# Statistics of the norm ahead of layer 1's router: row sum from the operation that makes x, variance by ScalarE's square with bias and sum

## The chip, the cores and the metric

The kernel runs on 1 core of one Trainium2 chip. The metric is the device time of one execution in microseconds (us). Each kernel is run several times and the median counts. The profile is of one further execution, whose own time is given beside its span. Engines are named as the profile names them: PE (matmul, with PEld for its weight loads), DVE (VectorE), ACT (ScalarE), POOL (GpSimd), SP (SyncE, which here only issues DMAs).

## The reference, cut to what matters

Two layers, each a graph attention over N = 2708 nodes with D = 256 features, followed by a mixture of experts in which each node goes to its two best experts. Layer 1 is the part that matters here:

```
x = x + L1_gnn(layernorm(x), adj, ...)        # out: 2708 x 256
n = layernorm(x)                              # (x - mean) / sqrt(var + 1e-5), per row
logits = n @ gate_w                           # 256 x 16 experts
top-2 experts and their softmax weights
moe = sum over both of weight * (relu(n @ w1[e]) @ w2[e])     # w1: 256 x 512, w2: 512 x 256
x = x + layernorm(n + moe) * gamma + beta
```

The change is in the second line: how the mean and the variance of a row of the new x are found.

## The kernel before, in words

The 2708 rows are 22 tiles of up to 128 rows (tiles 20 and 21 have 74). In layer 1 the attention is a product on PE: for each tile 44 matmuls at `att_ps` (L1772) with the mask, widened from 8 bits by POOL (L1620) or ACT (L1622), as weights. The order of tiles on PE is 20, 2 to 19, 21, after 0 and 1.

Around this product a planner orders everything at build time. `Clock` holds a list of generators ("pieces"). A piece yields an engine and an estimated time, or a `Mark` that another piece sets; `Clock.run` always lets the piece with the earliest start go on, and the order in which it does so is the order of instructions on every engine. On the chip each engine takes its instructions strictly in that order, and waits where an operand is not there yet. So a change of a piece's estimates or waits can move other pieces' instructions on every engine.

The pieces that matter here:

- `attention` issues the matmuls of L1772. A tile needs one of three accumulators, which `finish1` of an earlier tile gives back.
- `finish1(t)`: `inv` (L1982, DVE reads the sum from the accumulator), three activations (L1985, L1987, L1989, ACT), two DVE operations (L1991, L1993; the second frees the accumulator), and a square with sum (L1997, ACT).
- `points1(part)`: works on a part of tiles at once: (0-3), (4-5), (6-9), (10-11), (12-15), (16-17), (18-19), (20-21). Some fifty small DVE operations on 128 x n numbers (L379 to L396, about 0.2 us each when one waits for the other) with activations L2011, L2061, L2063 and L2070 between; then per tile the new x (L2090, DVE, 128 x 256) and its statistics (`ln_f1.stats`: `bn_stats` L481 and `bn_aggr` L482, DVE); then per part `var` (L379), nine steps of a reciprocal square root, `shift` (L391), and per tile the normalized row `xr` (L506, ACT), which is stored (L1020, a DMA by SP).
- `logits1(two)`: transposes of `xr` on PE (L515), a copy (L610, ACT), the gate product (L520, PE), and `logits` (L626, DVE).
- `route1(group)`, groups of tiles (0-5), (6-11), (12-17), (18-21): the top two per row (L648 to L667, DVE), ranks (L680 to L690, PE), numbering (L710 to L746, DVE), then `scatter1`, two indirect DMAs per tile by POOL that move `xr` to its experts' rows (L753), and `plan`, which finds which expert each block of 128 rows has (L881 to L948: `where` L925 by ACT, `hot_f` L933 by DVE, `bias_ps` L943 by PE). After the groups 1, 2 and 3 a plan is made; blocks 0 to 7 can start after group 1, blocks 8 to 19 after group 2.
- `stream`: 45 blocks of experts. SP fetches the block's rows (L850) and weights (L834, L838) in its own order, in which the stores of L1020 stand too. PE: transposes (L515), 16 steps of weight load and matmul at `hid_ps` (L972), and at `out_ps` (L987, L990). ACT: the copy `lo` (L1108) and four `ht` (L976). DVE: `yo` (L996). POOL adds `yo` to the sums in memory by an indirect DMA (L1001). PE's transposes, gate products and ranks of the last groups stand between the steps of the first blocks.

Before the change the part's statistics are these lines:

```
nc.vector.scalar_tensor_tensor(x1[:r, t, :], emb[:r, t, :], by[:r, q:q + 1], xq[q][:r, :D],
                               op0=OP.mult, op1=OP.add)
ln_f1.stats(x1[:r, t, :], t, r)
...
var = ts(ln_f1.mv[:, lo:hi, 1], LN_EPS, OP.add)
yield from rsqrt_steps(var, dev)
shift = ln_f1.shift(part)
```

Of the kernel before, what the change touches and what calls it, by code (L numbers as in the profile page):

```python
# [16 lines left out]
AF = mybir.ActivationFunctionType  # L17
OP = mybir.AluOpType
# [5 lines left out]
LN_EPS = 1e-5  # L24
# [123 lines left out]
def kernel(  # L148
# [25 lines left out]
    nc = tc.nc  # L174

    ctx.enter_context(tc.manual_schedule(engines={ET.PE, ET.Activation, ET.DVE, ET.SP}))
    N, D = x.shape
# [88 lines left out]
    def xr0_tile():  # L266
        return lasting.tile([P, RW], F32, name="xr", bufs=5)
# [95 lines left out]
    def stat(n, dtype=F32):  # L363

        count[0] += 1
        cols, bufs = next(of for of in STATS if n <= of[0])
        return sm.tile([P, cols], dtype, name=f"stat{count[0]}", tag=f"stat{cols}",
                       bufs=bufs)[:, :n]

    def kept(name, fill=None, cols=T):  # L370
        tl = sm.tile([P, cols], F32, name=name)
        if fill is not None:
            nc.gpsimd.memset(tl, fill)
        return tl

    def ts(a, s1, op0, s2=None, op1=None, dtype=F32):
        o = stat(a.shape[1], dtype)
        if op1 is None:
            nc.vector.tensor_scalar(o, a, s1, None, op0=op0)  # L379
        else:  # L380
            nc.vector.tensor_scalar(o, a, s1, s2, op0=op0, op1=op1)
        return o

    def tt(a, b, op, o=None):
        o = stat(a.shape[1]) if o is None else o
        nc.vector.tensor_tensor(o, a, b, op)
        return o

    def sts(a, s, op0, b, op1, o=None):
        o = stat(a.shape[1]) if o is None else o  # L390
        nc.vector.scalar_tensor_tensor(o, a, s, b, op0=op0, op1=op1)  # L391
        return o

    def recip(a):
        o = stat(a.shape[1])
        nc.vector.reciprocal(o, a)  # L396
        return o
# [6 lines left out]
    SMALL = "DVE", 0.11, 0.09  # L404
# [9 lines left out]
    def rsqrt_steps(v, o=None):  # L414

        yield SMALL
        shifted = ts(v.bitcast(I32), 1, OP.logical_shift_right, dtype=I32)
        yield SMALL
        y = ts(shifted, -1.0, OP.mult, float(0x5F3759DF), OP.add, dtype=I32).bitcast(F32)
        yield SMALL  # L420
        r = tt(v, y, OP.mult)
        yield SMALL
        r = tt(r, y, OP.mult)
        yield SMALL
        h = sts(r, -10.0 / 3.0, OP.add, r, OP.mult)
        yield SMALL
        y = sts(h, 5.0, OP.add, y, OP.mult)
        c = 0.375
        yield SMALL
        h = sts(v, -0.5 * c ** 3, OP.mult, y, OP.mult)  # L430
        yield SMALL
        h = tt(h, y, OP.mult)
        yield SMALL
        return sts(h, 1.5 * c, OP.add, y, OP.mult, o)
# [1193 lines left out]
    def xr_tile():  # L1628
        return side.tile([P, RW], F32, name="xr1", bufs=13)

    def fetch_row(tl, src, t, r):
        for lo, hi in parts_of_rows(r):
            nc.sync.dma_start(tl[lo:hi], src[t * P + lo:t * P + hi, :])
# [218 lines left out]

    emb = h_all[:, :, :D]
    emb_sq, sig_sq, common = kept("emb_sq", 1.0), kept("sig_sq", 32.0), kept("common")
    router1 = Router(1, E1, groups1, wg1, bg1, side)
    router1.fill()
    sums1 = [sums_d(f"sums1_{k}", zero=k == 1) for k in range(2)]
# [8 lines left out]
    x1 = emb  # L1866
    square = side.tile([P, D], BF16, name="square")
    ln_f1, ln_y = Norm("f1"), Norm("y")

    clock = Clock()  # L1870
# [14 lines left out]
    def group_of(two):  # L1885
        return next(g for g in groups1 if g[0][0] <= two[0][0] <= g[-1][0])

    def urgency(two):
        return 1 + groups1.index(group_of(two)) / len(groups1)
# [139 lines left out]
    def points1(part):  # L2029

        lo, n = part[0][0], len(part)
        hi = lo + n
        xq, xp_slots, x_at = [], [], [Mark() for _ in range(n // 2)]

        def fetch_x():
            for k in range(0, n, 2):
                xp_slots.append((yield from xps.get()))
                for t, r in part[k:k + 2]:
                    xq.append(xr0_tile())
                    fetch_row(xq[-1][:, :D], x_d, t, r)  # L2040
                clock.moved(x_at[k // 2], 0.9, 2.0)

        sq = emb_sq[:, lo:hi]
        v = stat(2 * n)
        yield SMALL
        nc.vector.tensor_scalar(v[:, :n], sq, MIN_NORM * MIN_NORM, None, op0=OP.max)
        yield SMALL
        nc.vector.tensor_scalar(v[:, n:], sq, 1.0, None, op0=OP.add)
        y = yield from rsqrt_steps(v)
        yield SMALL  # L2050
        roots = tt(v, y, OP.mult)
        yield SMALL
        u = tt(roots[:, :n], roots[:, n:], OP.add)
        log = yield from half_log(u)
        yield SMALL
        clock.start(fetch_x())
        inward = sts(log, 0.5 * LEAST, OP.max, y[:, :n], OP.mult)

        for q, (t, r) in enumerate(part):
            yield "ACT", 0.5  # L2060
            nc.scalar.activation(emb[:r, t, 1:], emb[:r, t, 1:], AF.Tanh, scale=inward[:r, q:q + 1])  # L2061
            yield "ACT", 0.7
            nc.scalar.activation(square[:r, 1:], emb[:r, t, 1:], AF.Square,  # L2063
                                 scale=0.5, bias=half[:r], accum_out=sig_sq[:r, t:t + 1])

        y = yield from rsqrt_steps(sig_sq[:, lo:hi])
        yield SMALL
        s_n, e = tt(sig_sq[:, lo:hi], y, OP.mult), stat(n)
        yield "ACT", 0.22
        nc.scalar.activation(e, s_n, AF.Exp)  # L2070
        yield SMALL
        ie = recip(e)
        yield SMALL
        sinh = tt(e, ie, OP.subtract)
        by = common[:, lo:hi]
        yield SMALL
        nc.vector.scalar_tensor_tensor(by, sinh, 0.25, y, op0=OP.mult, op1=OP.mult)
        yield SMALL
        cosh = tt(e, ie, OP.add)
        yield SMALL  # L2080
        ratio = recip(by)
        yield SMALL
        ratio = sts(cosh, 0.5, OP.mult, ratio, OP.mult)
        yield SMALL
        nc.vector.tensor_scalar(emb[:, lo:hi, 0], ratio, -1.0, None, op0=OP.add)
        for q, (t, r) in enumerate(part):
            if q % 2 == 0:
                yield x_at[q // 2]
            yield "DVE", 0.5
            nc.vector.scalar_tensor_tensor(x1[:r, t, :], emb[:r, t, :], by[:r, q:q + 1], xq[q][:r, :D],  # L2090
                                           op0=OP.mult, op1=OP.add)
            yield "DVE", 0.62
            ln_f1.stats(x1[:r, t, :], t, r)
            if q % 2:
                clock.set(xp_slots[q // 2])
        dev = ln_f1.rstd[:, lo:hi]
        yield SMALL
        var = ts(ln_f1.mv[:, lo:hi, 1], LN_EPS, OP.add)
        yield from rsqrt_steps(var, dev)
        yield SMALL  # L2100
        shift = ln_f1.shift(part)
        for q, (t, r) in enumerate(part):
            xr_slots[t] = yield from xrs.get()
            router1.rows[t] = xr_tile()
            yield "ACT", 0.6
            ln_f1.apply_s(router1.rows[t][:r, :D], x1[:r, t, :], t, r, shift[:, q:q + 1])
            experts1.store(t, r, router1.rows[t][:r, :D])
            if q % 2:
                clock.start(logits1(part[q - 1:q + 1], taken_at[t - 1]), urgency(part))
        if hi == group_of(part)[-1][0] + 1:  # L2110
            clock.start(route1(group_of(part)), urgency(part))

    def route1(group):
        g = groups1.index(group)
        for t, _ in group[::2]:
            yield taken_at[t]
        if g:
            yield routed_at[g - 1]
        yield from router1.pick(group, 0)
        yield from router1.pick(group, 1)  # L2120
        slot = yield from bank.get()
        yield "PE", 0.16 * len(group)
        router1.rank(group)
        yield from router1.number(group)
        clock.set(slot)
        upto = experts1.NB if group is groups1[-1] else early1.get(g)
        clock.start(scatter1(group, upto), urgency(group))
        if upto:
            yield from experts1.plan(upto, bank)
        clock.set(routed_at[g])  # L2130

    def scatter1(group, upto):
        for t, r in group:
            yield "POOL", 2.6
            router1.scatter(t, r)
            clock.set(xr_slots.pop(t))
        if upto:
            clock.set(experts1.scattered_at[upto], 3.5)
# [362 lines left out]
```

## Time and profile before

| what | value |
|---|---|
| median of 3 runs | 1139.43 us (1137.65 to 1140.55) |
| the profiled execution | 1135.28 us, of it the span 1133.6 us |
| PE busy | 1038.0 us (92%) |
| DVE busy | 542.4 us (48%) |
| ACT busy | 576.4 us (51%) |
| POOL busy | 368.5 us (33%) |
| layer 1's attention, 740 to 871 us: PE busy | 114.41 of 131 us |
| the change-over to the experts, 871 to 946 us: PE busy | 50.87 of 75 us |
| experts, 946 to 1105 us: PE busy | 152.07 of 159 us |

A row of the timeline gives start, duration, engine, line, operation, output and inputs, and in brackets how long the engine had been idle before it and what ended that. "Issue" is idle time that no recorded wait explains; "remote" is a wait for another engine whose work had long ended by the record. A row of the table of windows gives the stretch, its length, and for each engine its busy time (and instructions), then the granted clock of PE, the busy share of the DMA engines and GB/s. Shares of busy time over the whole span say little here: before 740 us other parts of the program run, which the change does not touch.

### The profile page before, as it was taken

Reading aid. Unit: us, or ns where it says so; the run is one execution under the profiler, and the core shown is the slowest. Engines: PE = TensorE matmul, PEld = TensorE weight load, DVE = VectorE, ACT = ScalarE, POOL = GpSimd, SP = SyncE. Lnnn points to the kernel's source line nnn. Section 1 sums busy time; section 2 is a strip of 40 time slices with the busy share of each in tenths; the row PEclk is TensorE's granted clock in tenths of the full one; section 3 lists DMA queues with packets and bytes.
Section 4 is the critical chain, followed back from the end, with each engine's and each line's share of the span. In section 5 each row is a group of like instructions: output and inputs, shape, how many; then the busy total and the mean of one; then the engine's idle time right before and its main releaser. Section 6 shows DMA issues by size and latency. Waiting matters only on the chain. (4 is left out here: it accounts for less than half of the span.)

```text
span 1133.6 us, 21472 instructions
## 1 busy us (share of the span) xinstructions
PE 1038.0 (92%) x6707; PEld 921.6 (81%) x6707; DVE 542.4 (48%) x2210; ACT 576.4 (51%) x1602; POOL 368.5 (33%) x425
## 2 busy tenths in 40 slices
PE   5999999998989999999999999898985967999994
PEld 3788888887879999998999854898984856999882
DVE  7778888887421111101110347577865553122257
ACT  4866667664524444444444346545653633544454
POOL 7531112111242222112213361352534155434350
PEclk9999999999999999999999999997996788999997
DMA  9965454431889999999899959401114656785893
GB/s 289 282 248 177 137 176 152 170 95 55 306 252 283 331 323 321 325 305 319 257 312 331 356 155 279 160 1 51 53 61 130 179 138 144 162 203 105 227 292 129
DMA packets 161862, 234.38 MB, mean 207 GB/s; under 512 B 10891, under 2 KB 137798, under 8 KB 159032
## 3 DMA queue, kind: packets, MB, share of 16 engines
q1 hardware_dynamic: 143356, 209.90, 57.0%
q0 software_dynamic: 18384, 23.03, 10.6%
q8 instruction: 56, 0.92, 0.3%
q14 instruction: 66, 0.54, 0.2%
HBM read 205.54 MB, written 54.59 MB: 229 GB/s over the span
## 5 line engine op out<-in xcount | busy, mean ns | idle before, releaser
L996 DVE TENSOR_SCALAR yo<-out_ps,w 128x256 f32<-128x256 f32 x89 | 43.0, 483 | 383.3 <-PE out_ps L990 376.2
L1346 PE MATMUL att_ps<-g_all,z 128*128 128x257 f32 (+3 forms) x968 | 223.6, 383 | 0.0
L1346 PEld LDWEIGHTS att_ps<-g_all,z 128*128 128x128 f32 (+3 forms) x968 | 174.9, 186 | 29.5 <-issue 2.9
L990 PE MATMUL out_ps<-room,ht 128*128 128x256 f32 x840 | 191.4, 380 | 0.0
L972 PEld LDWEIGHTS hid_ps<-xt,room 128*128 128x128 f32 x1504 | 176.9, 194 | 9.3 <-issue 3.7
L972 PE MATMUL hid_ps<-xt,room 128*128 128x128 f32 x1504 | 178.9, 278 | 5.4 <-issue 2.7
L990 PEld LDWEIGHTS out_ps<-room,ht 128*128 128x128 f32 x840 | 155.5, 191 | 20.0
L1332 ACT ACTIVATE zr<-e_bc,minus_one,g_all 128x256 f32<-128x256 f32 (+3 forms) x242 | 130.2, 591 | 44.4 <-DVE z L1335 44.3
L1772 PE MATMUL att_ps<-half,wide_mask 128*128 128x258 f32 (+1 forms) x962 | 131.3, 295 | 14.9 <-issue 8.1
L976 ACT ACTIVATE ht<-hid_ps,w_t 128x128 f32<-128x128 f32 x376 | 128.6, 364 | 30.3 <-PE hid_ps L972 11.7
L1001 POOL DMA_INDIRECT sums<-yo,xg x43 | 66.8, 1554 | 233.8 <-DVE side L964 188.5
L1772 PEld LDWEIGHTS att_ps<-half,wide_mask 128*128 128x128 f32 (+1 forms) x962 | 124.5, 198 | 19.0 <-issue 14.8
L753 POOL DMA_INDIRECT rows_d<-xr,place x88 | 91.8, 1043 | 119.7 <-DVE xr L497 66.4
L1335 DVE SCALAR_TENSOR_TENSOR z<-zr,mask_t 128x256 f32<-128x256 f32 (+3 forms) x242 | 97.8, 424 | 31.1 <-ACT zr L1332 17.4
L976 ACT ACTIVATE ht<-hid_ps,w1x 128x128 f32<-128x128 f32 x180 | 65.1, 366 | 83.5 <-PE hid_ps L972 67.5
L1001 POOL DMA_INDIRECT sums<-yo,xr x42 | 65.7, 1564 | 117.0 <-DMA sums<-yo,xr 40.6
L966 ACT ACTIVATE w<-xg,side 128x1 f32<-128x1 f32 x43 | 12.7, 294 | 165.8 <-DVE side L964 165.8
L1620 POOL CAST wide_mask<-mask_t 128x1408 fp32r<-128x1408 fp8e4 x34 | 47.0, 1387 | 95.8 <-PE att_ps L1772 95.8
L972 PE MATMUL hid_ps<-lo,wide_mask 128*128 128x128 f32 x368 | 51.2, 297 | 3.5 <-ACT lo L1108 3.0
L972 PEld LDWEIGHTS hid_ps<-lo,wide_mask 128*128 128x128 f32 x368 | 49.5, 211 | 5.7 <-ACT lo L1108 3.9
L515 PE MATMUL tr_ps<-ident,xr 128*128 128x128 f32 (+1 forms) x214 | 39.6, 297 | 14.6 <-ACT xr L506 12.9
L515 PEld LDWEIGHTS tr_ps<-ident,xr 128*128 128x128 f32 (+1 forms) x214 | 28.1, 154 | 22.1 <-ACT xr L506 14.2
(334 smaller groups left out, 1442.6 us busy)
## 6 DMA issues: line engine op xcount, KB each, us to landing
room<-in_L_ffn_W_dram SPq DMA_DIRECT2D x94, 1024.0 KB
room<-in_adj_dram SPq DMA_DIRECT2D x20, 1354.0 KB
wide_mask<-in_L_ffn_w_dram SPq DMA_DIRECT2D x46, 512.0 KB
room<-in_L_ffn_w_dram SPq DMA_DIRECT2D x22, 512.0 KB
mask_t<-in_L_ffn_w_dram SPq DMA_DIRECT2D x22, 512.0 KB
rows_d<-nobody SPq DMA_DIRECT2D x1, 7511.0 KB
rows_d<-nobody SPq DMA_DIRECT2D x5, 1295.0 KB
sums<-nobody SPq DMA_DIRECT2D x2, 2944.0 KB
```

Source lines behind the costliest of these rows:

```text
L515: nc.tensor.transpose(ps[:, c, :r], src[:, c * P:(c + 1) * P], ident[:r, :r])
L753: ins = nc.gpsimd.indirect_dma_start(out=self.rows_d[:, :], in_=self.rows[t][:r], in_offset=None, out_offset=bass.IndirectOffsetOnAxis(ap= ...
L972: nc.tensor.matmul(ps[:, :P], w1_b[:, c, f * P:(f + 1) * P], xt[:, c, :], start=(c == 0), stop=(c == DC - 1))
L976: nc.scalar.activation(ht[:, f, :], ps[:, :P], self.func, bias=self.bias[:, f, b:b + 1])
L990: nc.tensor.matmul(ps[:, :D], ht[:, f, :], self.rooms[b % self.deep][1][:, f, :], start=False, stop=(f == self.FC - 1))
L996: nc.vector.tensor_scalar(yo, ps[:, :D], w, None, op0=OP.mult)
L1001: ins = nc.gpsimd.indirect_dma_start(out=self.sums[k][:, :], in_=yo, in_offset=None, out_offset=bass.IndirectOffsetOnAxis(ap=self.rows.pop ...
L1332: nc.scalar.activation(zr[:k, :n], e_bc[:k, lo:lo + n], AF.Relu, bias=minus_one[:k], scale=g_all[:k, j, D + 1:D + 2])
L1335: nc.vector.scalar_tensor_tensor(z[:k, :n], zr[:k, :n], 1.0, mask_t[:k, j // 2, lo:lo + n, j % 2], op0=OP.add, op1=OP.mult)
L1346: nc.tensor.matmul(accs[i][:r, :D + 1], z[:k, q * P:q * P + r], g_all[:k, j, :D + 1], start=(j == 0), stop=(j == LAST))
L1620: nc.gpsimd.tensor_copy(m, src)
L1772: nc.tensor.matmul(accs[i][:, :D + 2], last_masks[i][:k] if late else wide_masks[i, j % 2][:k, j // 2, :], half_k[:k, j, :], start=(j == 0 ...
```

## The change

The operation that makes the new x (L2090) now also writes out the sum of its row (`accum_out=x_sum`). After each pair of tiles one small DVE operation makes minus the mean (`x_off`). A new piece, `squares1`, then has ACT square the row with the bias `x_off` and sum it (`x_var`, the variance times 256), one activation per tile, the output of which goes to the scratch tile `square`. `var` waits for the marks of all pairs, and `shift` is a product of two small operands. `bn_stats` and `bn_aggr` fall away for these 22 tiles. The estimate for L2090 is 0.58 in place of 0.5, and 0.62 for the statistics is replaced by 0.7 on ACT per tile.

```
+    x_sum, x_off, x_var = kept("x_sum", 0.0), kept("x_off", 0.0), kept("x_var", 1.0)
...
+        dev, squared = ln_f1.rstd[:, lo:hi], [Mark() for _ in range(n // 2)]
         for q, (t, r) in enumerate(part):
             if q % 2 == 0:
                 yield x_at[q // 2]
-            yield "DVE", 0.5
+            yield "DVE", 0.58
             nc.vector.scalar_tensor_tensor(x1[:r, t, :], emb[:r, t, :], by[:r, q:q + 1], xq[q][:r, :D],
-                                           op0=OP.mult, op1=OP.add)
-            yield "DVE", 0.62
-            ln_f1.stats(x1[:r, t, :], t, r)
+                                           op0=OP.mult, op1=OP.add, accum_out=x_sum[:r, t:t + 1])
             if q % 2:
                 clock.set(xp_slots[q // 2])
-        dev = ln_f1.rstd[:, lo:hi]
-        yield SMALL
-        var = ts(ln_f1.mv[:, lo:hi, 1], LN_EPS, OP.add)
+                yield SMALL
+                nc.vector.tensor_scalar(x_off[:, t - 1:t + 1], x_sum[:, t - 1:t + 1], -1.0 / D, None,
+                                        op0=OP.mult)
+                clock.start(squares1(part[q - 1:q + 1], squared[q // 2]), urgency(part))
+        for mark in squared:
+            yield mark
+        yield SMALL
+        var = ts(x_var[:, lo:hi], 1.0 / D, OP.mult, LN_EPS, OP.add)
         yield from rsqrt_steps(var, dev)
         yield SMALL
-        shift = ln_f1.shift(part)
+        shift = tt(x_off[:, lo:hi], dev, OP.mult)
...
+    def squares1(two, mark):
+        for t, r in two:
+            yield "ACT", 0.7
+            nc.scalar.activation(square[:r], x1[:r, t, :], AF.Square, bias=x_off[:r, t:t + 1],
+                                 accum_out=x_var[:r, t:t + 1])
+        clock.set(mark, clock.HANDOVER)
```

## The prediction

> **What bounds the kernel now.** I first read the chain of waits that ended last. From 990 us on it is PE's experts and the adds behind them, in an order that the change leaves alone, so whatever delays the first full stretch of experts (945.82 us) comes through to the end one for one. Then the table of windows, to see where PE is not busy before that.
>
> ```profile
> 770.00:780.00 10.00, 5.59 (x36) 5.19 (x35) 9.48 (x45) 3.73 (x10) 3.06 (x2) 0.80 0.20 66
> 780.00:790.00 10.00, 10.00 (x49) 10.00 (x49) 3.55 (x22) 5.90 (x13) 0.00 (x0) 0.51 0.01 2
> ...
> 871.00:946.00 75.00, 50.87 (x334) 45.52 (x333) 44.24 (x277) 30.34 (x95) 26.45 (x31) 0.77 0.61 156
> ```
>
> PE loses 4.4 us in the first window and then works at half clock (0.51) through the second. In the change-over DVE is busy 44 of 75 us, ACT 30. Neither is full, so busy time that moves from one to the other is worth nothing by itself: only chains of waits count. The timeline of PE names them.
>
> ```profile
> 776.82 1.18 PE L515 MATMUL tr_ps<-ident,xr 128*128 128x128 f32 x4 [4.41 <-ACT xr L506]
> 834.40 0.77 PE L1772 MATMUL att_ps<-half,wide_mask 128*128 128x258 f32 x2 [2.78 <-DVE inv L1982]
> 879.78 2.16 PE L515 MATMUL tr_ps<-ident,xr 128*128 128x128 f32 x8 [8.53 <-ACT xr L506]
> 926.35 1.88 PE L943 MATMUL bias_ps<-hot_f,w1x 16*128 16x12 f32 x8 [8.33 <-issue]
> 943.95 0.27 PE L680 MATMUL rank_ps<-hot,tri 128*128 128x128 bf16 x1 [3.57 <-DVE hot L667]
> 945.82 0.58 PE L972 MATMUL hid_ps<-lo,wide_mask 128*128 128x128 f32 x1 [0.52 <-issue]
> ```
>
> Two of the five waits are for `xr`, the end of the norm that is changed. The other three hang on DVE's and ACT's order. So the latency from the new x to `xr` counts, part by part, and what DVE's order puts in between.
>
> **The prices.** The timelines of DVE, POOL and ACT give what the operations cost.
>
> ```profile
> 517.67 0.42 DVE L1504 SCALAR_TENSOR_TENSOR junk<-att_x,a_j 128x256 f32<-128x256 f32 x1
> 518.01 0.08 DVE L1504 DVE_READ_ACCUMULATOR junk<-att_x,a_j 128x1 f32 x1
> 518.01 0.42 DVE L1504 SCALAR_TENSOR_TENSOR junk<-att_x,a_j 128x256 f32<-128x256 f32 x1
> ...
> 769.86 0.45 DVE L2090 SCALAR_TENSOR_TENSOR h_all<-h_all,common,xr 128x256 f32<-128x256 f32 x1
> 770.34 0.43 DVE L481 BATCH_NORM_STATS2 bn<-h_all 128x6 f32<-128x256 f32 x1
> 770.91 0.90 DVE L2090 SCALAR_TENSOR_TENSOR h_all<-h_all,common,xr 128x256 f32<-128x256 f32 x1
> 773.57 0.53 DVE L379 TENSOR_SCALAR stat<-mv_f 128x4 f32<-128x4 f32 x1
> ...
> 825.49 0.17 DVE L1982 RECIPROCAL inv<-att_ps 128x2 f32<-128x2 f32 x1 [4.58 <-remote]
> ```
>
> ```profile
> 769.90 1.63 POOL L1620 CAST wide_mask<-mask_t 128x1408 fp32r<-128x1408 fp8e4 x1 [1.38 <-PE att_ps L1772]
> 772.55 1.52 POOL L1620 CAST wide_mask<-mask_t 128x1408 fp32r<-128x1408 fp8e4 x1 [1.02 <-PE att_ps L1772]
> ```
>
> ```profile
> 855.20 0.51 ACT L2063 ACTIVATE square<-h_all,half 128x255 bf16<-128x255 f32 x1
> 855.62 0.19 ACT L2063 ACTIVATION_READ_ACCUMULATOR square<-h_all,half 128x1 f32 x1
> ...
> 869.16 0.19 ACT L948 COPY w1x<-bias_ps 128x32 f32<-128x32 f32 x1 [7.31 <-remote]
> ```
>
> Removed: 22 `bn_stats` and `bn_aggr`. A tile of L2090 and both took 1.05 (769.86 to 770.91); with the sum written out, two of this shape start 0.34 apart (L1504), so I take 0.4 per tile. DVE loses 22 x 0.65 = 14.3 and gains 11 `x_off` of 0.17, about 1.9. ACT gains 22 x 0.51 = 11.2 (L2063, its read of the sum included). For a part of four tiles the serial 4.2 us on DVE become some 2.0, then 0.2, then the squares, which run behind the first pair's `x_off`. That alone would bring `xr` forward by about 1 us in a part of four and leave it about even in a part of two. What the built order of the changed kernel puts around it is dearer:
>
> (a) **Tiles 0-3.** DVE's order becomes x0, x1, `x_off`, x2, x3, `x_off`, then the ten steps of part (4-5) that before ran interleaved, and only then `var`, nine steps with the x of tile 4 among them, and `shift`. Dependent steps are 0.2 us apart. Unhindered from 768.77: second `x_off` at 770.7, ten steps 2.0, then 2.7: 775.4 against 776.07 before, a gain of 0.6. But POOL's casts of 769.90 and 772.55 hold DVE operations up: the third L2090 took 0.90 and L379 0.53, while `bn_stats` inside the first cast took its usual 0.43. x3 then comes at 771.5, `x_off` at 772.1, eight of the ten steps behind the second cast at 773.9: 775.6, plus 2.5: 778.1, so +2.0; with `x_off` held once more +2.8. I take +2.0, since x3 falls at the place where the row at 770.91 was held. PE waits for this at 776.82, and the operation that frees tile 10's accumulator stands behind it too.
>
> [...]
>
> The half clock may last 3.4 us longer behind a longer wait, worth 1.7; I leave that to the range. [...]
>
> (b) **Tiles 6-11.** `var` of 6-9 now stands behind `inv` of tile 15, which DVE reached at 825.49 after 4.58 idle, and behind part (10-11)'s way to x10 (827.79). From there x10, nine steps, x11 and `shift` are 3.1: 830.9, and the first pair of `xr` is out at 832.0. Before, those `xr` were out by 824.5. PE's order places their transposes 22 matmuls later (2.7 us at 0.122 each): it is there at 828.8 and waits 3.2. In return the 2.78 at 834.40 goes: the operation that frees tile 14's accumulator no longer stands behind four `logits`. At that point the old kernel had done 2.0 of transposes and gates that the new one still has to do: 832.2 + 2.0 against 834.4, even. Then group 1's rank comes 14 matmuls later (1.7), its scatter too, and the copy at 869.16, which comes 2 us after the last scatter. Less 1.0, as `inv` of tile 21 no longer waits for PE (0.97 idle at 871.28): +0.7, bounds -2.8 and +3.
>
> (c) **Tiles 12-15.** No casts now. From 872.60: second `x_off` at 874.5; 19 steps of the next two parts at 0.11 (two chains interleaved): 876.6. The squares end at 875.9, hidden under those steps; were those gone, the squares would hold `var` by 1.2. Then 2.8: 879.4 against 879.09, and ACT starts `xr`: +0.4, bounds -0.7 and +1.3. Queued behind it on SP: the stores of tiles 12 and 13, and block 0's fetch.
>
> (d) **Tiles 16-17.** Their squares follow four `xr` on ACT. The second copy L610 now stands behind `lo` of block 0, and `xr` of 17 behind four `ht` and the next `lo`; their gate follows the outputs of block 0. `logits` about 900 instead of 897.1: +3. The numbering of this group gets shorter: two L2090 with their statistics and a `yo` (2.5 in all) leave it. +0.5, bounds 0 and +3.
>
> (e) **Group 2's plan.** Half the hidden steps of block 6 (1.0) now stand behind `bias_ps`, where before PE idled 8.33: +1.0, bounds 0 and +1. The squares of 20 and 21 cost nothing: `var` at 931 is ahead of the `yo` at 932.50 that held the nine steps anyway, and `xr` of 20 (934.92) waits for its turn behind `ht`. Without that cover they cost 0.7.
>
> Sum: 2.0 + 0.7 + 0.4 + 0.5 + 1.0 = 4.6. The profiled execution's 1135.28 (span 1133.6 and 1.7 around it) becomes 1139.9. The median is 4.15 above that execution: 1144.0.
>
> **The rivals.** *Faster:* PE's wait for the freed accumulator (2.78) vanishes and nothing takes its place, with the 3.4 us of half clock behind it (1.7), and the shorter numbering (2.5) counts in full with (d) otherwise even: -7.0, and +0.4 for (c): 1132.8. It decides at one point: whether `xr` of 6 and 7 is out when PE gets to it at 828.8. For it: DVE, the busiest engine beside PE (91 of 131 us in the attention), is relieved. Against: the built order hangs `var` on `inv` of tile 15.
>
> *No change:* POOL's scatters set the pace. The waits of 7.31 and 8.33 end near the end of a run of 12 scatters of 1.27 each, whatever was ready before. If DVE's numbering, shorter by 2.5, starts them no later, and (a) is at its free end, the sum is -0.6 + 0.7 + 0.4 - 1.0 = -0.5 for (a) to (d), and with the 1.0 of (e) +0.5: 1139.9.
>
> *Much slower*, the upper end of my own case: 2.8 + 1.7 + 3 + 1.3 + 3 + 1 = 12.8, 1152.
>
> **How the numbers follow.** What a measurement here can tell from no change is about 0.3%, 3.4 us. My case gets 0.50, no change 0.22, faster 0.28. The likeliest is 1144.0, its own range 1141 to 1151. The range 1132 to 1151 takes in the faster rival's time and leaves what lies beyond both ends out, some 2 in 10.
>
> **What would show it.** In the profile after: PE's first wait for `xr` grows from 4.41 to 6 or more; the wait on `inv` L1982 gives way to one on `xr` near 829; the squares at 0.51; 945.82 becomes about 950. Wrong if that first wait shrinks, or if PE meets the transposes of tiles 6 and 7 without waiting.

## The result, and the profile after

The changed kernel takes 1142.66 us (median of 17 runs, 1139.26 to 1145.87), the kernel before in the same session 1140.38 us (median of 17, 1133.79 to 1144.39). The ratio is 1.0024, with an interval of 1.0009 to 1.0040: slower, by about 2.7 us (2.3 by the two medians, since the ratio is not their quotient), and so close to 0.3% that it is at the edge of what a measurement of this kernel can tell from no change. The forecast was 1144.0. Ratios and medians here are of the fast runs alone, because one execution of each kernel took longer at a lower granted clock (before 1153.13 us at 0.949, after 1235.69 at 0.829).

The profiled execution of after is also the median one, 1142.66 us with a span of 1140.7. That of before (1135.28, span 1133.6) lies near the low end of its own runs. The two spans differ by 7.1 us, then, where the medians differ by 2.3, and the traces cannot be subtracted as they are. A part of the difference lies ahead of everything that the change touches: 1.5 us up to 723 us, and 1.7 us in a stretch of half clock behind that (3.41 us from 723.54), which the trace of before has not. I leave both out below.

The timeline of PE after the change, at the places that the prediction names:

```profile
781.06 1.18 PE L515 MATMUL tr_ps<-ident,xr 128*128 128x128 f32 x4 [5.59 <-ACT xr L506]
...
832.58 1.18 PE L515 MATMUL tr_ps<-ident,xr 128*128 128x128 f32 x4 [3.58 <-ACT xr L506]
883.25 2.16 PE L515 MATMUL tr_ps<-ident,xr 128*128 128x128 f32 x8 [19.81 <-ACT xr L506]
924.70 1.89 PE L972 MATMUL hid_ps<-lo,room 128*128 128x128 f32 x8 [3.50 <-issue]
949.67 0.26 PE L680 MATMUL rank_ps<-hot,tri 128*128 128x128 bf16 x1 [3.58 <-DVE hot L667]
951.49 2.93 PE L972 MATMUL hid_ps<-lo,wide_mask 128*128 128x128 f32 x12 [0.46 <-ACT lo L1108]
```

The reader should see four things. The first wait for `xr` grew from 4.41 to 5.59. The 2.78 on `inv` is gone, and 3.58 on `xr` stands at 832.58 in its place. The wait at 883.25 looks twice as long as before only because the last attention matmuls, which broke it up before, came earlier; its end counts, 3.5 us later than 879.78, and 3.2 of these lie ahead of the change. And the 8.33 of idle time ahead of `bias_ps` is gone: 3.50 stand ahead of the first half of block 6's hidden steps, `bias_ps` follows without a wait, and the other half comes behind it. The forecast's 945.82 "becomes about 950" is 951.49, or 948.3 without the 3.2.

The table of windows for the same three stretches:

```profile
770.00:780.00 10.00, 5.46 (x45) 5.26 (x44) 9.48 (x46) 7.05 (x23) 4.34 (x3) 0.91 0.05 13
780.00:790.00 10.00, 8.94 (x61) 8.70 (x62) 4.75 (x26) 7.21 (x18) 0.00 (x0) 0.75 0.17 55
...
871.00:946.00 75.00, 51.47 (x313) 46.07 (x314) 35.60 (x254) 37.36 (x121) 23.75 (x25) 0.73 0.54 146
```

In the change-over DVE is busy 35.60 us where it was busy 44.24, ACT 37.36 instead of 30.34. The work did move, and the stretch did not get shorter. The second row has the surprise: PE's clock averages 0.75 from 780 to 790, where it was 0.51. Over the whole span DVE's busy time fell from 542.4 to 533.3 us and ACT's rose from 576.4 to 589.0.

To follow the time I cut each trace at events that both kernels share: ACT's first `xr` (L506), the first scatter of each group, the first new x of tile 12, the first `xr` of tile 12, the end. A stage is the time from one to the next, in us.

| stage | before | after | difference |
|---|---|---|---|
| A: attention of layer 1 (from 721.94 / 723.47) to the first `xr`, without the half clock ahead | 54.23 | 55.22 | +0.99 |
| B: to the first scatter of group 0 | 31.61 | 27.50 | -4.11 |
| C: to the first scatter of group 1 | 44.16 | 46.77 | +2.61 |
| D: to the new x of tile 12 | 20.66 | 19.01 | -1.65 |
| E: to the `xr` of tile 12 | 6.53 | 8.92 | +2.39 |
| F: to the first scatter of group 2 | 31.01 | 32.46 | +1.45 |
| G: to the first scatter of group 3 | 38.29 | 39.21 | +0.92 |
| H: to the end | 185.17 | 186.43 | +1.26 |
| sum | 411.66 | 415.52 | +3.86 |

The sum is close to the 4.6 forecast; the rows that make it are not all the forecast's rows. There is one trace of before on this sort of chip, so a row of 1 us or less is near what one trace can show.

### The profile page after: what moved, and what is told of

Same layout as the page of the kernel before. It is cut to its first block, busy times and chain, and to the rows that moved or that the text cites. A ratio compares the mean times of both kernels' runs of the same rounds, so it can differ in the third digit from the quotient of the medians.

```text
span 1140.7 us, 21508 instructions
## 1 busy us (share of the span) xinstructions
PE 1036.2 (91%) x6707; PEld 918.7 (81%) x6707; DVE 533.3 (47%) x2199; ACT 589.0 (52%) x1646; POOL 368.8 (32%) x428
## 5 line engine op out<-in xcount | busy, mean ns | idle before, releaser
L1772 PE MATMUL att_ps<-half,wide_mask 128*128 128x258 f32 (+1 forms) x962 | 126.4, 290 | 7.3 <-DVE stat L396 2.1
L1772 PEld LDWEIGHTS att_ps<-half,wide_mask 128*128 128x128 f32 (+1 forms) x962 | 121.1, 194 | 10.0 <-issue 5.7
L515 PEld LDWEIGHTS tr_ps<-ident,xr 128*128 128x128 f32 (+1 forms) x214 | 28.0, 153 | 44.5 <-ACT xr L506 31.1
```

What stands on the lines that cost most here:

```text
L515: nc.tensor.transpose(ps[:, c, :r], src[:, c * P:(c + 1) * P], ident[:r, :r])
L1772: nc.tensor.matmul(accs[i][:, :D + 2], last_masks[i][:k] if late else wide_masks[i, j % 2][:k, j // 2, :], half_k[:k, j, :], start=(j == 0 ...
```

## The experiments

The experiments ran on three chips, and these turned out to be of two sorts. On one of them, as in the first pair, before takes 1140 to 1144 us; on the two others 1108 to 1109. Each sort was seen in two sessions only, and no run shows that the chip itself makes the difference; "sort of chip" is a name for it. Ratios are always against before on the same chip, and I say which sort it was.

**1. Both kernels again.** No edit: `before_again` is the kernel before, `after_again` the changed one.

> The kernel before, run once more, for a second trace of it. The two traces differ by 3.05 us when layer 1's first wait for xr begins (772.41 and 775.47), where the change has done nothing yet, and by 0.12 us at the first scatter (807.78 and 807.90); PE ran at half clock for about 13.7 us in the trace before and 6.5 us in the one after. If the length of the half clock belongs to the wait that comes before it (4.4 us), it is near 13.7 again. If it is chance, it differs, and then neither the 3.05 us nor their loss belongs to the change. First wait for xr: 4.4 +- 0.3 either way; scatters of group 1 start 44 us after those of group 0 (851.94 - 807.78).

> The changed kernel once more, timed on this chip beside the kernel before. All theories: ratio about 1.002 (1.001 to 1.004), its first wait for xr 5.6 +- 0.3, the wait for xr of tiles 6 and 7 near 3.6, scatters of group 1 46.8 us after those of group 0 (854.67 - 807.90 in the first trace; 44.2 in the kernel before). If the half clock is chance, its length differs from 6.5.

This chip was of the shorter sort. Before took 1108.32 (17 runs; the profiled execution 1111.04), after 1119.71 (3 runs), ratio 1.0119 (1.0085 to 1.0153), where about 1.002 was expected. The change costs five times as much here. In the traces C costs +5.15 without the half clock in it (6.83 us of it in after, which cost 3.42, and none in before), and E +4.79; the other stages are as in the first pair within 1 us, but for H (-0.63).

The timelines show what differs. First before, on this chip:

```profile
857.00 0.19 ACT L948 COPY w1x<-bias_ps 128x32 f32<-128x32 f32 x1 [0.72 <-PE bias_ps L943]
867.90 0.16 DVE L391 SCALAR_TENSOR_TENSOR stat<-mv_f,rstd_f 128x4 f32<-128x4 f32 x1
872.12 0.48 DVE L2090 SCALAR_TENSOR_TENSOR h_all<-h_all,common,xr 128x256 f32<-128x256 f32 x1 [1.86 <-DMA xr<-x_d]
```

Then after, on this chip:

```profile
858.70 0.19 ACT L948 COPY w1x<-bias_ps 128x32 f32<-128x32 f32 x1 [0.73 <-PE bias_ps L943]
865.84 0.96 POOL L753 DMA_INDIRECT rows_d<-xr,place  x1 [0.30 <-issue]
872.55 0.48 DVE L2092 SCALAR_TENSOR_TENSOR h_all<-h_all,common,xr 128x256 f32<-128x256 f32 x1 [4.48 <-DMA xr<-x_d]
872.96 0.16 DVE L386 TENSOR_TENSOR stat<-x_off,rstd_f 128x4 f32<-128x4 f32 x1
```

The plan's copy L948 comes right behind its matmuls, 7 us before the last scatter is issued. On the first chip it came after the burst:

```profile
868.85 0.96 POOL L753 DMA_INDIRECT rows_d<-xr,place  x1 [0.30 <-issue]
871.85 0.19 ACT L948 COPY w1x<-bias_ps 128x32 f32<-128x32 f32 x1 [8.69 <-remote]
```

That late hand-over stands in both kernels (idle ahead of the copy: 7.31 us in before, 8.69 in after), and by my reading of the traces it hides part of what the change delays. The other thing to see is a step that the prediction did not have: in after the new x of tile 16 (L2092) stands ahead of `shift` of 12-15 in DVE's queue, and waits there for its load of x, 4.48 us, where in before `shift` (L391, at 867.90) was done 4 us ahead of that x (L2090, at 872.12). On the first chip it is the same with 2.34:

```profile
881.99 0.48 DVE L2092 SCALAR_TENSOR_TENSOR h_all<-h_all,common,xr 128x256 f32<-128x256 f32 x1 [2.34 <-DMA xr<-x_d]
882.40 0.16 DVE L386 TENSOR_TENSOR stat<-x_off,rstd_f 128x4 f32<-128x4 f32 x1
```

**2. The new operations in the old plan (`old_order`).** The estimates and hand-overs of before are kept, so that the orders of PE, POOL and SP are those of before (but for POOL's fills of the new tiles at the program's start):

```
-            yield "DVE", 0.58
+            yield "DVE", 0.5
             ... the new x with its row sum
+            yield "DVE", 0.62
             ... behind each pair: x_off, then at once
+                for u, s in part[q - 1:q + 1]:
+                    nc.scalar.activation(square[:s], x1[:s, u, :], AF.Square, bias=x_off[:s, u:u + 1], ...)
```

> The new operations in the old plan: PE, POOL and SP get exactly the order of the kernel before, DVE too but for the replaced operations, and the squares stand in ACT's queue where the plan of before had the second statistics of a pair. Theory order (my prediction's (b), (d), (e): what the new plan puts in between is what costs): the shorter serial part comes through, about 1 us in a part of four on the path twice (tiles 0-3, 12-15), a part of two even: ratio to before 0.998 to 1.000, and the scatters of group 1 start 44 us or less after those of group 0. Theory operations (casts holding the new DVE operations, the hand-over to ACT and back): the loss stays, 1.002, and the first wait for xr is 5.6 again. Theory scatters (the bursts set the pace): 1.000.

Ratio 1.0018 (1.0000 to 1.0035), 1109.99 against 1108.32, same chip as 1. So most of the 1.2% there is the plan and not the operations; and the operations by themselves gain nothing. Why not is on the timelines of DVE and ACT:

```profile
863.01 0.17 DVE L2095 TENSOR_SCALAR x_off<-x_sum 128x2 f32<-128x2 f32 x1
865.92 0.68 DVE L381 TENSOR_SCALAR stat<-x_var 128x4 f32<-128x4 f32 x1 [2.74 <-ACT square L2098]
```

```profile
862.90 0.51 ACT L2098 ACTIVATE square<-h_all,x_off 128x256 bf16<-128x256 f32 x1
863.41 0.45 ACT L1986 ACTIVATE lo<-att_ps,inv 74x256 f32<-74x256 f32 x1
863.90 0.42 ACT L1988 ACTIVATE xn<-lo 74x256 f32<-74x256 f32 x1
864.35 0.42 ACT L1990 ACTIVATE lo<-lo 74x256 f32<-74x256 f32 x1
864.67 0.49 ACT L2098 ACTIVATE square<-h_all,x_off 128x256 bf16<-128x256 f32 x1
865.28 0.51 ACT L2098 ACTIVATE square<-h_all,x_off 128x256 bf16<-128x256 f32 x1
```

The last `x_off` is out at 863.01, but `var` waits 2.74 for the squares: each takes 0.63 with its read, and three activations of `finish1` stand between them. DVE is relieved, and ACT's queue gives the time back.

**3. The changed kernel without `x_off` (`no_off`).** The square takes -256 x plus the row sum, so it needs nothing from DVE but the sum (the edit is against after):

```
-            nc.scalar.activation(square[:r], x1[:r, t, :], AF.Square, bias=x_off[:r, t:t + 1], ...)
+            nc.scalar.activation(square[:r], x1[:r, t, :], AF.Square, scale=-float(D), bias=x_sum[:r, t:t + 1], ...)
-        var = ts(x_var[:, lo:hi], 1.0 / D, OP.mult, LN_EPS, OP.add)
+        var = ts(x_var[:, lo:hi], 1.0 / D ** 3, OP.mult, LN_EPS, OP.add)
-        shift = tt(x_off[:, lo:hi], dev, OP.mult)
+        shift = sts(x_sum[:, lo:hi], -1.0 / D, OP.mult, dev, OP.mult)
```

> As the changed kernel, but x_off is gone: ScalarE squares (row sum - 256 x), with scale -256 and the sum as bias, var is that over 256 cubed, and shift takes the sum times -1/256. 11 DVE operations of 0.17 fewer, and the squares of a pair wait for one operation less; the plan shifts by a few instructions, and the loads of x16 and x17 move ahead of 13 other DMAs on SP. Theory order: the plan still has var behind the next part's steps, so most stays: ratio to before 1.001 to 1.003. Theory operations: the first wait for xr shrinks by the x_off that a cast held and two steps of 0.2, 5.6 to 5.0, and the ratio to 1.0005 to 1.0015. In both the wait of 2.34 us for the load of x16, behind which the shift of tiles 12-15 stood, is gone (xr of 12-15 up to 2 us sooner).

Ratio 1.0128 (1.0100 to 1.0157; 4 runs), same chip: no better than after. Stage E is 12.11 against 12.54, and the x of tile 16 still waits 4.32 for its load ahead of `shift`, a wait that was expected to go. The eleven small operations are worth nothing that these runs can tell; the place of `shift` is not touched by taking them out.

**4. After a third time, on a chip like the first (`after_third`).** No edit.

> The changed kernel once more, as the measure for the other runs of this call: two chips have shown it 1.0024 and 1.0119 of the kernel before. If the shift of tiles 12-15 waits behind x16, and x16 for its load (2.34 us on the one, 4.48 on the other), the loss goes with that wait: a chip where the copy of the biases (L948) comes within 1 us of its matmuls gives about 1.012, one where it comes 8 us late, 2 us after the last scatter, about 1.002.

Ratio 1.0019 (0.9987 to 1.0051), 1145.34 (10 runs) against 1143.42 (29 runs). The stages repeat those of the first profile within 0.6 us, A at 55.19. So 1.002 and 1.012 go with the two sorts of chip and not with chance between executions.

**5. The old operations in the new plan (`new_plan`).** The orders of PE, POOL and SP are those of after; behind each L2092 stand `bn_stats` and `bn_aggr`, and the squares are only estimates on ACT's clock:

```
-                                           op0=OP.mult, op1=OP.add, accum_out=x_sum[:r, t:t + 1])
+                                           op0=OP.mult, op1=OP.add)
+            ln_f1.stats(x1[:r, t, :], t, r)
-            nc.scalar.activation(square[:r], x1[:r, t, :], AF.Square, ...)   # the yield stays
-        var = ts(x_var[:, lo:hi], 1.0 / D, OP.mult, LN_EPS, OP.add)
+        var = ts(ln_f1.mv[:, lo:hi, 1], LN_EPS, OP.add)
```

> The old operations in the new plan, the other half of old_order: the planner orders as for the changed kernel (its estimates for the squares included), so PE, POOL and SP get exactly the changed kernel's order, but the statistics are bn_stats and bn_aggr behind each x again, and the squares and x_off are not there. Theory plan (what stands between the operations costs, above all x16 ahead of the shift of tiles 12-15): as slow as the changed kernel, within 0.3% of it; 1.008 to 1.013 of the kernel before on a chip like the one of old_order. Theory operations: as the kernel before, 1.000 +- 0.002.

Ratio 1.0105 (1.0067 to 1.0144), 1154.0 against 1143.42, same chip as 4. Against after on that chip it is 8.7 us more. A grows by another 1.7 us:

```profile
786.88 1.18 PE L515 MATMUL tr_ps<-ident,xr 128*128 128x128 f32 x4 [7.23 <-ACT xr L506]
```

The new plan with the old operations costs 10.6 us, and the new operations win 8.7 of that back on this sort of chip. This answers the expectation that new_plan would be within 0.3% of the changed kernel: it is 0.8% slower. In the old plan the new operations win nothing (2, on the other sort, and 7). The change's loss is the sum of a dearer order and cheaper operations that almost pay for it.

**6. `shift` of 12-15 ahead of the x of tile 16 (`shift_first`, and on the other sort of chip `shift_again`).** One added wait in the planner:

```
+    hold_behind, shift_at = {16: 12}, [Mark() for _ in range(T)]
...
             if q % 2 == 0:
                 yield x_at[q // 2]
+            if not q and lo in hold_behind:
+                yield shift_at[hold_behind[lo]]
...
         shift = tt(x_off[:, lo:hi], dev, OP.mult)
+        clock.set(shift_at[lo])
```

> The changed kernel with one edge more: x16 may be given out only after the shift of tiles 12-15. On PE only the gate products of two tiles move by 8 instructions. Theory x16 (the shift stands behind an operation that waits 4.48 us for a load): DVE's wait for the load comes behind the shift, xr of 12 starts 4.5 us sooner on a chip like that of old_order (about 7.5 us behind x12 in place of 12.5), and 4 to 6 us of the loss go: 1.006 to 1.008; on a chip like the first, 2.3 us, so 1.000 to 1.001. Theory that the rest of the plan costs as much (6-11 late, PE's order): 1.010 or more.

> shift_first once more, to narrow its interval (0.9946 to 1.0003) and, on a chip where the biases' copy is not late, to see the other size of its gain. Theory x16: near 0.9975 on a chip with the late copy; on the other kind the changed kernel's 1.0119 less 4.5 to 6 us, 1.006 to 1.008.

On the chip of 4: 1141.19 against 1143.42, ratio 0.9975 (0.9946 to 1.0003), where the unedited change had 1.0019. On the other sort: 1.0036 (1.0021 to 1.0052), where it had 1.0119 (on another chip of that sort). The expectations were 1.000 to 1.001 and 1.006 to 1.008, so both gains are larger than `shift` alone was to give. DVE's timeline of `shift_first`, then of `shift_again`:

```profile
884.19 0.15 DVE L386 TENSOR_TENSOR stat<-x_off,rstd_f 128x4 f32<-128x4 f32 x1
...
885.84 0.48 DVE L2096 SCALAR_TENSOR_TENSOR h_all<-h_all,common,xr 128x256 f32<-128x256 f32 x1 [1.05 <-DMA xr<-x_d]
```

```profile
866.60 0.16 DVE L386 TENSOR_TENSOR stat<-x_off,rstd_f 128x4 f32<-128x4 f32 x1
...
871.11 0.48 DVE L2096 SCALAR_TENSOR_TENSOR h_all<-h_all,common,xr 128x256 f32<-128x256 f32 x1 [3.96 <-DMA xr<-x_d]
```

The wait for the load is still there, but `shift` no longer stands behind it: stage E falls to 6.42 and 7.71, what before has (6.53 and 7.75). This shows the cause of E. E alone is not the whole gain: between `after_third` and `shift_first` E falls by 2.53 and F by 2.67, while G takes 1.67 back; why F falls was not followed.

**7. The row sum alone in the old plan (`old_sum`).** The order of before, no `x_off`, each square directly behind its x:

```
+            nc.scalar.activation(square[:r], x1[:r, t, :], AF.Square, scale=-float(D), bias=x_sum[:r, t:t + 1], ...)
+            yield "DVE", 0.62
-                nc.vector.tensor_scalar(x_off[:, t - 1:t + 1], x_sum[:, t - 1:t + 1], -1.0 / D, None, op0=OP.mult)
```

> The version that the runs point to: the plan of before as in old_order, no x_off (the bias of the square is the row sum itself, scale -256), and each tile's square given to ScalarE right behind its x, ahead of the three activations of finish1 that stood between the pairs. var waits for the last square only: x of the fourth tile ends 1.7 us after the first one's start, its square 1.1 later, so var about 3.0 us behind the first x in place of 4.34 (bn) and 4.85 (old_order); in a part of two 2.2 against 2.25. Theory chain (the way from x to xr is on the path at tiles 0-3 and 12-15): 1 to 1.3 us each, ratio 0.997 to 0.999. Theory that a cast or another wait takes it back: 0.999 to 1.002, and the first wait for xr stays at 4.2 or more.

Ratio 1.0031 (1.0008 to 1.0055), 1146.15 against 1143.42, on the chip of 4. `var` of 12-15 still waits for ACT, and the idea that giving each square out at once would end that wait falls:

```profile
880.96 0.17 DVE L381 TENSOR_SCALAR stat<-x_var 128x4 f32<-128x4 f32 x1 [3.13 <-ACT square L2093]
```

**8. Both repairs, and the middle part too (`shift_no_off`, `mid_ahead`).** `shift_no_off` is the edit of 6 with that of 3. `mid_ahead` adds to it that the squares of 6-9 are given out at once:

```
+                if lo == 6:
+                    for u, s in part[q - 1:q + 1]:
+                        nc.scalar.activation(square[:s], x1[:s, u, :], AF.Square, scale=-float(D), ...)
+                    clock.set(squared[q // 2], 0.9)
+                else:
+                    clock.start(squares1(part[q - 1:q + 1], squared[q // 2]), urgency(part))
```

> shift_first without x_off (the square's bias is the row sum, its scale -256). By the first wait for xr of no_off against the changed kernel (0.3 us sooner behind the start of layer 1) and the shorter chain at tiles 12-15, 0.2 to 0.8 us less than shift_first: 0.996 to 0.998 on a chip with the late copy. Theory that the plan's shifts decide: anywhere within 0.3% of shift_first.

> shift_no_off with the squares of tiles 6-9 given out at once behind their x, so that ScalarE does them ahead of the widening that waits for PE (3.89 us in the changed kernel's trace), and var of 6-9 comes ahead of inv of tile 15. Theory (b) of the prediction (var of 6-9 is late behind inv of 15, and group 1's scatters with it, 2.6 us on the first chip): scatters of group 1 start 44 to 45 us behind those of group 0 in place of 46.9, and 1 to 2.6 us go: 0.994 to 0.996 on a chip with the late copy. Against: the numbering of group 1 and its plan move too (the x of tiles 12-15 now stand ahead of hot_f), which may take it back: 0.997 to 1.001.

Ratios 1.0026 (1.0008 to 1.0043) and 1.0011 (0.9990 to 1.0031), on the shorter sort of chip, beside `shift_again` at 1.0036. Taking `x_off` out gains nothing that these intervals can tell. Of the re-planned versions `mid_ahead` is the first that can't be told from before there. Its C is 0.6 us shorter than that of `shift_no_off`, and of that the half clock (1.71 against 0) is more than all, so the emission of the squares did not pay in that stage. The edit also moved more than it was meant to: the x of tile 12 comes 0.60 behind the first scatter of group 1 instead of 8.97 (stage D), and G takes 36.30 instead of 27.89. The ratio of `mid_ahead` is therefore not the price of that one emission.

**9. Half the scatters of group 1 (`scatter_fewer`).** The kernel before, with the second expert's rows of tiles 6 to 11 not moved (6 of 12 scatters left out):

```
-            for k in range(2):
+            for k in range(1 if t in self.once else 2):
...
+    router1.once = range(6, 12)
```

> The kernel before with half of group 1's scatters: the second expert of the rows of tiles 6-11 gets no row (6 indirect DMAs of 12 left out), all else in the same order. Theory scatters (on a chip with the late copy the hand-over to ScalarE waits until the run of scatters is over): the burst ends 7.6 us sooner, the copy of the biases comes 2.0 to 2.3 us behind its end again, so 7.6 sooner, and x12 with it (13 us behind the first scatter in place of 20.7). Theory that another wait holds the copy: it stays 17 us behind the first scatter. On a chip without the late copy: copy 0.04 us behind the matmuls of the biases, x12 10.7 behind the first scatter as before.

One run, 1114.22 us, and the chip was of the shorter sort, on which the copy does not wait for the burst in the first place. POOL's and ACT's timelines:

```profile
855.09 0.96 POOL L755 DMA_INDIRECT rows_d<-xr,place  x1 [0.30 <-issue]
856.06 0.19 ACT L950 COPY w1x<-bias_ps 128x32 f32<-128x32 f32 x1 [0.72 <-PE bias_ps L945]
```

The copy is 0.04 us behind the end of its matmuls (856.02). The run says nothing on the chips where the copy is late. That the burst holds it up there is not shown by an experiment. It rests on the traces alone: copy 2.0 to 2.4 us behind the end of the last scatter in all six traces from such chips.

## Why the prediction was right or wrong, step by step

**The direction and the size were right, and the size was luck in good part.** Ratio 1.0024 is +2.7 us; the trace without what lies ahead of the change gives +3.86; forecast +4.6. Term by term, A and B together are -3.1 where (a) had +2.0, and E, F and H together are 5.1 where (c) and (d) had 0.9; these two misses cancel to within 1 us. Two small numbers of it were off as well: two squares in a row stand 0.63 apart and not 0.51, and 879.4 against 879.09 is +0.3, not +0.4. Neither decides the sum.

**(a) Tiles 0-3: mechanism right, size half, and its other side missed.** The cast held x3, the third row here, as forecast. DVE, then POOL:

```profile
772.86 0.48 DVE L2092 SCALAR_TENSOR_TENSOR h_all<-h_all,common,xr 128x256 f32<-128x256 f32 x1
773.26 0.08 DVE L2092 DVE_READ_ACCUMULATOR h_all<-h_all,common,xr 128x1 f32 x1
773.26 1.58 DVE L2092 SCALAR_TENSOR_TENSOR h_all<-h_all,common,xr 128x256 f32<-128x256 f32 x1
```

```profile
772.95 1.61 POOL L1620 CAST wide_mask<-mask_t 128x1408 fp32r<-128x1408 fp8e4 x1 [1.35 <-PE att_ps L1772]
```

The two tiles start 0.40 apart until the cast, as the prices had it, and then one takes 1.58. The wait grew by 1.18 and A by 0.99 (1.35 on the other sort of chip), not 2.0, and the "6 or more" was 5.59. The ends of A, ACT's first `xr`, first before and then after:

```profile
776.17 2.08 ACT L506 ACTIVATE xr<-h_all,stat,rstd_f 128x256 f32<-128x256 f32 x4
```

```profile
780.40 2.08 ACT L506 ACTIVATE xr<-h_all,stat,rstd_f 128x256 f32<-128x256 f32 x4 [0.20 <-DVE stat L386]
```

The failed step is the half clock. The prediction left it to the range that it could last 3.4 us longer, as long as the stretch of half clock behind the 2.78 on `inv` in before (834.12 to 837.53); it was far shorter, in all nine traces of the new plan. Before, PE starts its first transposes at 776.82 and is at half clock until 789.75, 12.9 us; after, it starts at 781.06 and has its full clock back at 784.98, 3.9 us later. The 9.0 us less at half clock are worth 4.5 of work, and B fell by 4.11. So by the end of B the change is ahead by 3.1 us, where I had it behind by 2.0. It is no accident of one execution: all five traces of the old plan show a stretch of 13.65 us of half clock there (before, `before_again`, `old_order`, `old_sum`, `scatter_fewer`), all nine of the new plan one of about 6.8, on both sorts of chip and with either kind of statistics. In all of them the stretch begins within PE's wait.

The length goes with the order of PE's work. Behind the wait the old order has 8 transposes, 10 attention matmuls and 16 of the 16-column gate products in small groups; the new one has 8 transposes and 20 attention matmuls before the first gate product, and the clock is back before that one starts. PE before, then after:

```profile
780.38 1.72 PE L520 MATMUL gate_ps<-wg,xts 128*128 128x16 f32 x8
...
782.51 1.73 PE L520 MATMUL gate_ps<-wg,xts 128*128 128x16 f32 x8
784.08 8.02 PE L1772 MATMUL att_ps<-half,wide_mask 128*128 128x258 f32 x44
```

```profile
784.47 1.91 PE L1772 MATMUL att_ps<-half,wide_mask 128*128 128x258 f32 x12
786.22 1.86 PE L520 MATMUL gate_ps<-wg,xts 128*128 128x16 f32 x16
```

When in the stretch PE starts is not what decides: half clock had begun 1.72 us ahead of PE's start in `old_order` and 1.85 in `after_third`, and lasted 13.65 and 6.83. But PE's wait was longer too in every trace of the new plan (5.59 to 7.23, against 4.25 to 4.44), and no run has the one without the other. That the narrow products keep the clock down is a reading of this, which no run tried. The next wait for `xr` (832.58 in after) speaks for it, since the order of PE there is nearly the same in all of the new plan. Among the traces that have half clock there: where 1 to 3 gate products started in the first 3.41 us of half clock, it ended with them (after, `new_plan`, `shift_again`); where 6 and 8 did, it lasted 6.83 (`after_again`, `no_off`); but in `shift_no_off` it ended after 3.41 with 6. Without the gain in B the change would have stood near +8, by my estimate (3.86 + 4.5).

**(b) Tiles 6-11: right on this sort of chip.** Forecast +0.7, measured C + D = +0.96. Its steps stand in the timeline of DVE and ACT nearly as written: `inv` of tile 15 at 825.52, `shift` at 831.73 (forecast 830.9), PE's wait 3.58 (forecast 3.2), D shorter by 1.65 (forecast 1.0).

```profile
825.52 0.17 DVE L1983 RECIPROCAL inv<-att_ps 128x2 f32<-128x2 f32 x1 [2.50 <-remote]
828.41 0.17 DVE L381 TENSOR_SCALAR stat<-x_var 128x4 f32<-128x4 f32 x1
831.73 0.16 DVE L386 TENSOR_TENSOR stat<-x_off,rstd_f 128x4 f32<-128x4 f32 x1
```

On the other sort of chip the term fails: C costs +5.15 there with the half clock taken out. C of after is nearly the same on both (45.1 and 44.5, without half clock); C of before is 42.5 on the first chip and 39.4 on the other, since there the late `inv` and the wait behind it are nearly absent (0.86 and 0.26 of idle time, against 4.58 and 2.78). Where the old kernel lost nothing, the new one had nothing to give back.

**(c) Tiles 12-15: the failed term.** Forecast +0.4 (-0.7 to +1.3), measured +2.39, and +4.79 on the other chips. I counted the steps between the x and `shift` by what they take, and read that the next part's x stood among them, but not what that x waits for: its load. The chain itself was fine. Counted from the new x of tile 12 (872.60 in the forecast, 873.68 measured), `var` stood 4.0 behind it, as forecast, and the last of the nine steps 5.8 (879.49), so that `shift` could have ended about 6.1 behind it (forecast 6.8); there DVE stopped for 2.34. Experiment 6 puts `shift` ahead of this wait, and E goes back to 6.42.

**(d) Tiles 16-17.** F is +1.45 (forecast +0.5, bounds 0 and +3), and both of its parts were mis-sized. The `logits` of these tiles, before and after:

```profile
897.10 0.26 DVE L626 TENSOR_TENSOR logits<-gate_ps,bg 128x16 f32<-128x16 f32 x2 [0.31 <-PE gate_ps L520]
```

```profile
902.08 0.26 DVE L626 TENSOR_TENSOR logits<-gate_ps,bg 128x16 f32<-128x16 f32 x2 [0.31 <-PE gate_ps L520]
```

They come 17.97 and 19.48 behind the `xr` of tile 12, +1.51 where +3 was forecast. From there to the first scatter both kernels take the same (13.04 and 12.98), so the gain of 2.5 from a shorter numbering is not in this stage.

**(e) Group 2's plan.** G is +0.92 (forecast +1.0), but not by the forecast's way. Behind the scatter `bias_ps` comes 4.8 us sooner than before (11.45 in place of 16.21). Behind `bias_ps` PE then has the other half of block 6's hidden steps, 2.08 long at half clock, and a wait of 3.59 for ACT's `ht` that the prediction did not have:

```profile
926.51 1.88 PE L943 MATMUL bias_ps<-hot_f,w1x 16*128 16x12 f32 x8
928.32 2.08 PE L972 MATMUL hid_ps<-lo,room 128*128 128x128 f32 x8
933.98 0.69 PE L515 MATMUL tr_ps<-ident,xr 128*128 128x128 f32 x2 [3.59 <-ACT ht L976]
```

These 5.7 take the 4.8 back and 0.9 more: the number was met by luck. **H** was taken to follow one for one, and grew by 1.26. Its order is unchanged and on the other sort it shrank by 0.63. Its cause stays open; in the other traces of this sort H is 185.4 to 188.0, so it may be no more than the spread between executions.

**The rivals.** The faster one did not happen: PE met `xr` of tile 6 too early, the point that it named. "No change" named the late hand-overs under scatter bursts, and by experiments 1 and 4 the change costs 1.2% where they are absent and 0.2% where they are present. That they are what hides the rest is not shown, since the run that took scatters away met the other sort of chip. They did not hide the whole.

**What would have been better.** `shift_first` beats both kernels by its median on the first sort of chip (0.9975), but its interval reaches 1.0003, and on the other sort it loses 0.36%. No version here beat before on both.

## What to carry to other kernels

When a change gives operations to another engine, read the built order for what now stands ahead of each step of the chain, and price that neighbour by what it waits for, a load above all (2.34 and 4.48 us here), not by its own 0.4 us. Moving work off an engine that is 48% busy did not pay here, because the queue of the engine that took it was not free at that moment: DVE lost 9.1 us of busy time and ACT gained 12.6, and in the old order `var` waited 2.7 to 3.1 us for the squares. Test a re-planned kernel both ways, new operations in the old order and old operations in the new one; here neither alone was faster, for different reasons.

## What the runs showed of the hardware that was not expected

- PE's half clock came in stretches of 3.41 us or a multiple of it: 3.41, 6.83, 10.24, 13.65 and 30.72 in the trace of before, 3.41, 6.83, 13.65 and 34.13 in that of after (the last stretch of each is cut off by the end). Behind the first `xr` it was two or four times 3.41, with the plan's order, and in stage C none to two, varying between traces. Counted from the start of PE's work behind that wait, the full clock was back after 3.9 us in after and after 12.9 in before, with PE busy all along.
- Two sorts of chip (or session, which no run separates): the same program takes 1140 to 1144 us on one and 1108 to 1109 on the other. On the longer sort ACT's copy of PE's result during a burst of scatters comes some 2 us after the burst's end, 8.6 us behind its matmuls in before and 10 in after; on the other it comes 0.04 us behind them. What differs stays open.
- A DVE operation beside a cast on POOL was held as in the prediction's rows, and the effect is not small: 1.58 us for an operation that takes 0.48 to 0.53 in the other 21 tiles of after, beside a cast of 1.61.
